# An attention kernel whose product with the values goes to 64x32 array tiles, from a rearranged weight tile

## The chip, the cores and the metric

One core of a Trainium2 chip runs the kernel. The metric is the device time of one execution in microseconds (us), as the median of several runs. The engines are TensorE (PE, with its weight loads shown apart as PEld), VectorE (DVE), ScalarE (ACT), GpSimd (POOL) and SyncE (SP, which only issues transfers here).

## The reference

A cross-attention block in float32. Two layer norms are modulated by a condition vector (adaLN), then queries come from x, keys and values from a context of 64 rows per batch element, and the block ends in a projection and a residual sum:

```
x: (16, 1024, 512)   context: (16, 64, 512)   16 heads of 32
xq  = LN(x)       * (1 + scale_q)  + shift_q      # scale, shift from silu(cond) @ Wss
xkv = LN(context) * (1 + scale_kv) + shift_kv
q = xq @ Wq + bq ;  k, v = split(xkv @ Wkv + bkv)
p = softmax(q k^T / sqrt(32))                     # over the 64 keys
out = x + (p v) @ Wp + bp
```

## The kernel before, in words

The 16 x 1024 rows are cut into 32 blocks (`NB`) of 512 rows, two to a batch element (`BPB`). Keys and values are made for the 16 batch elements in two context groups, A and B, in a prologue. Dense products (q, k, v, projection) are computed in 128x128 tiles by a scheme with seven products where a plain one has eight (`seven`, `product`). What belongs to a block i:

- `score_products` (L659-666): the scores of one half z of the keys (32 of 64) for all heads, K = 32, in 32x32 array tiles into two pairs of PSUM banks, `ps`. The pool `ps_s` holds just these two pairs, so the next score group, or the product with the values, needs both free again.
- `maximum` (L683, DVE), `copied` (L692, ACT: a pair of banks into the SBUF tile `s_tiles[i, z]`), `maxima` (L703, L712, tile mb on DVE), `subtract` (L725, POOL), `weights` (L731, ACT, the exponential in place).
- `total` (L765, POOL: both halves added), `row_total` (L770, DVE, tile lt), `inverse_rows` (L782-790): the reciprocal (L785) on DVE, then one transfer ltd<-lt to DRAM (L788) and four transfers vr<-ltd back (L790), all on SP; `spread_rows` (L796) spreads vr into vb.
- `mix` (L818-834): the product with the values into `po`, which takes the two bank pairs of `ps_s`. For each half z, each of four groups c of heads and each of four heads r in a group, one matmul with 32 rows (keys) and 32 columns; z = 1 accumulates on z = 0. So 32 matmuls, two instructions each. V lies in `V_A` or `V_B` with 32 partitions for each c, filled by `value_move` with transfers from `stage`.
- `divided` (L814, DVE, ot<-po,vb), `row_sums` (L928-938, POOL) and then the projection (`product`, L958).

The input of a later block is normalised by `q_stats`, `q_scale` (L310-319: five small ACT instructions, then four on POOL), `hidden` (L344), `turn` (L375) and `move` (L397: 16 transfers xt<-ht on SP), then `scale_features` (L455) and `feature_sums` (L506).

The order is written out by hand: a prologue, then a loop for i from 3 to 29 and a tail. Each engine works through its own instructions in that order. One pass of the loop holds, among others, `scores(i, 0, crossed=True)` (the two copies in swapped order), `scores(i, 1)`, `mix(i - 1)`, `weights(i, 0)`, `query_out(n, 6)`, `weights(i, 1)`, `total(i)`, `query_out(n, 7)`, `query_out(n, 3)`, `row_total(i)`, `inverse_rows(i)`, `move(i + 3)` and `q_scale(i + 4)`, with n = i + 1.

Of the kernel before, what the change touches and what calls it, by code (L numbers as in the profile page):

```python
# [15 lines left out]
P = 128  # L16
# [4 lines left out]
def cross_attention_block(  # L21
# [369 lines left out]
    def move(i, two=False):  # L391

        ht = ht_tiles.pop(i)
        xt = features_tile(i)
        for k in range(4):
            for g in range(4):
                (nc.gpsimd if two and g % 2 else nc.sync).dma_start(  # L397
                    xt[32 * k : 32 * k + 32, g],
                    ht[32 * g : 32 * g + 32, k].rearrange("p c t b -> p c (t b)"),
                )  # L400
# [258 lines left out]
    def score_products(i, z):  # L659
# [98 lines left out]

    sum_tiles, lt_tiles, vt_rows = {}, {}, {}
# [22 lines left out]
    def inverse_rows(i):  # L782

        lt = lt_tiles.pop(i)
        nc.vector.reciprocal(lt, lt)  # L785
        v = small.tile([P, NC, NJ], F32, tag="vr", name=f"vr_{i}")
        d = dram.tile([NC, 32, HPC, NJ], F32, tag="lt", name=f"ltd_{i}")
        nc.sync.dma_start(d.rearrange("c a r j -> (c a) r j"), lt)  # L788
        for r in range(HPC):
            nc.sync.dma_start(v[32 * r : 32 * r + 32], d[:, :, r, :].rearrange("c a j -> a c j"))  # L790
        vt_rows[i] = v
# [26 lines left out]
    def mix(i, apart=True, ks=(None,) * NC):  # L818
# [7 lines left out]
        else:  # L826
            po = [bank(f"po_{i}_{c}", ks[c]) for c in range(NC)]
            po_tiles[i] = po
        for z in range(2):
# [261 lines left out]
    q_stats("B", (2,))  # L1091
    turned_products()
    turned_scaled(3)
    load_x(1)
    q_stats("B", (1,))
    load_x(2)
    turned_scaled(2)
    context_out("A", "v", 7)
    context_product("A", "k", 5)
    column_sums("q", w_q_sb, w_q_sums, (0,))  # L1100
    column_sums("q", w_q_sb, w_q_sums, (1,))
    context_out("A", "v", 5)
    load_projection()
    q_stats("B", (3,))
    turned_scaled(0)
    context_product("A", "k", 4)
    context_out("A", "k", 4)
    q_scale("B")
    context_out("A", "k", 5)
    q_stats(1, (0,))  # L1110
    turned_scaled(1)
    hidden("B", (3,))
    context_product("A", "v", 3)
    hidden("B", (2,))
    context_product("A", "k", 3)
    hidden("B", (1,))
    turned_features("B", 1)
    turned_features("B", 3)
    q_stats(1, (1,))
    hidden("B", (0,))  # L1120
    feature_sums(0, nc.gpsimd, (0,))
    turned_features("B", 0)
    feature_sums(0, nc.gpsimd, (1,))
    turned_features("B", 2)
    column_sums("q", w_q_sb, w_q_sums, (2,))
    context_out("A", "k", 3)
    q_stats(1, (3,))
    query_product(0, 1)
    feature_sums(0, nc.gpsimd, (2,))
    modulated("B", 0, 0, nc.scalar)  # L1130
    q_stats(1, (2,))
    q_scale(1)
    query_seed(0)
    modulated("B", 1, 0, nc.vector)
    context_product("A", "v", 4)
    context_out("A", "v", 3)
    hidden(1, (0,))
    modulated("B", 0, 0, nc.vector)
    hidden(1, (1,))
    turn(1, (0,))  # L1140
    load_x(3)
    hidden(1, (2,))
    load_projection_bias()
    query_product(0, 2)
    turn(1, (1,))
    turn(1, (2,))
    hidden(1, (3,))
    column_sums("q", w_q_sb, w_q_sums, (3,))
    turn(1, (3,))
    q_stats(2, (0,))  # L1150
    feature_sums(0, nc.gpsimd, (3,))
    q_stats(2, (3,))
    context_out("A", "v", 4)
    move(1, two=True)
    query_out(0, 2)
    query_product(0, 6)
    query_out(0, 6)
    modulated("B", 0, 1, nc.scalar)
    modulated("B", 1, 1, nc.vector)
    modulated("B", 0, 1, nc.vector)  # L1160
    modulated("B", 1, 1, nc.scalar)
    context_product("B", "k", 1)
    query_product(0, 5)
    feature_sums("B", nc.gpsimd, (0,))
    context_out("B", "k", 1)
    query_product(0, 7)
    q_stats(2, (1,))
    modulated("B", 1, 0, nc.scalar)
    q_stats(2, (2,))
    feature_sums("B", nc.gpsimd, (1,))  # L1170
    query_out(0, 7)
    query_added(0, 5)
    context_product("B", "k", 2)
    query_product(0, 4)
    q_scale(2)
    q_stats(3, (0,))
    query_product(0, 3)
    context_out("B", "k", 2)
    q_stats(3, (2,))
    hidden(2, (0,))  # L1180
    hidden(2, (3,))
    feature_sums("B", nc.gpsimd, (2,))
    context_product("B", "k", 6)
    feature_sums("B", nc.gpsimd, (3,))
    hidden(2, (2,))
    query_out(0, 3)
    hidden(2, (1,))
    query_added(0, 4)
    q_stats(3, (1,))
    q_stats(3, (3,))  # L1190
    context_product("B", "k", 7)
    turn(2, (0,))
    turn(2, (1,))
    score_products(0, 0)
    scale_features(1, (1,))
    turn(2, (2,))
    context_out("B", "k", 6)
    context_out("B", "k", 7)
    value_move("A", 0)
    maximum(0, 0, 0)  # L1200
    context_product("B", "k", 5)
    scale_features(1, (0,))
    turn(2, (3,))
    copied(0, 0, 1)
    scale_features(1, (2,))
    maximum(0, 0, 1)
    context_product("B", "k", 4)
    copied(0, 0, 0)
    load_x(4)
    q_scale(3)  # L1210
    score_products(0, 1)
    scale_features(1, (3,))
    query_product(1, 1)
    context_out("B", "k", 5)
    context_out("B", "k", 4)
    context_product("B", "k", 3)
    maximum(0, 1, 0)
    maximum(0, 1, 1)
    maxima(0)
    move(2)  # L1220
    hidden(3, (0,))
    query_seed(1)
    context_out("B", "k", 3)
    feature_sums(1, nc.gpsimd, (0,))
    hidden(3, (2,))
    hidden(3, (1,))
    query_product(1, 2)
    feature_sums(1, nc.gpsimd, (1,))
    query_out(1, 2)
    copied(0, 1, 0)  # L1230
    feature_sums(1, nc.gpsimd, (2,))
    q_stats(4, (0,))
    subtract(0, zs=(0,))
    copied(0, 1, 1)
    q_stats(4, (2,))
    query_product(1, 6)
    context_product("B", "v", 1)
    turn(3, (0,))
    query_product(1, 7)
    turn(3, (1,))  # L1240
    value_move("A", 1)
    hidden(3, (3,))
    context_out("B", "v", 1)
    load_x(5)
    query_out(1, 6)
    query_out(1, 7)
    query_product(1, 5)
    weights(0, 0)
    query_added(1, 5)
    turn(3, (2,))  # L1250
    q_stats(4, (1,))
    subtract(0, zs=(1,))
    feature_sums(1, nc.gpsimd, (3,))
    weights(0, 1)
    context_product("B", "v", 2)
    scale_features(2, (3,))
    context_product("B", "v", 6)
    turn(3, (3,))
    scale_features(2, (2,))
    total(0)  # L1260
    scale_features(2, (0,))
    q_stats(4, (3,))
    context_out("B", "v", 2)
    q_scale(4)
    move(3)
    query_product(1, 3)
    query_product(1, 4)
    query_added(1, 4)
    context_out("B", "v", 6)
    query_out(1, 3)  # L1270
    scale_features(2, (1,))
    score_products(1, 0)
    row_total(0)
    copied(1, 0, 0)
    feature_sums(2, nc.gpsimd, (0,))
    maximum(1, 0, 1)
    context_product("B", "v", 5)
    maximum(1, 0, 0)
    inverse_rows(0)
    context_product("B", "v", 7)  # L1280
    nc.gpsimd.tensor_tensor(b_diff, b_second, b_first, ALU.subtract)
    context_out("B", "v", 7)
    copied(1, 0, 1)
    hidden(4, (1,))
    feature_sums(2, nc.gpsimd, (1,))
    score_products(1, 1)
    hidden(4, (2,))
    hidden(4, (0,))
    maximum(1, 1, 0)
    maximum(1, 1, 1)  # L1290
    maxima(1)
    query_product(2, 1)
    copied(1, 1, 0)
    context_out("B", "v", 5)
    copied(1, 1, 1)
    feature_sums(2, nc.gpsimd, (2,))
    scale_features(3, (3,))
    context_product("B", "v", 4)
    mix(0)
    q_stats(5, (0,))  # L1300
    turn(4, (0,))
    turn(4, (1,))
    feature_sums(2, nc.gpsimd, (3,))
    context_product("B", "v", 3)
    context_out("B", "v", 3)
    subtract(1, zs=(1,))
    subtract(1, zs=(0,))
    spread_rows(0)
    scale_features(3, (0,))
    query_seed(2)  # L1310
    query_product(2, 2)
    query_product(2, 6)
    biased(0, 2)
    context_out("B", "v", 4)
    hidden(4, (3,))
    query_out(2, 2)
    query_out(2, 6)
    query_product(2, 7)
    query_product(2, 5)
    weights(1, 1)  # L1320
    q_stats(5, (3,))
    query_out(2, 7)
    load_residual(0)
    divided(0)
    weights(1, 0)
    product(0, 1)
    query_added(2, 5)
    value_move("B", 0)
    product(0, 2)
    scale_features(3, (1,))  # L1330
    row_sums(0, 0)
    scale_features(3, (2,))
    q_stats(5, (1,))
    q_stats(5, (2,))
    query_product(2, 3)
    value_move("B", 1)
    total(1)
    turn(4, (2,))
    query_out(2, 3)
    load_x(6)  # L1340
    weight_sums(0)
    added(0, 1)
    added(0, 2)
# [305 lines left out]
```

## Time and profile before

| | |
|---|---|
| median of 3 runs (lowest, highest) | 1018.99 us (1018.93, 1021.01) |
| the profiled execution | 1021.49 us, span 1019.7 us, granted TensorE clock 0.999 |
| busy in the span | PE 1007.1 us, DVE 864.3, POOL 808.1, ACT 637.6 |
| moved by transfers | 149.82 MB, mean 147 GB/s |

The span runs from the first to the last instruction; the profiled execution's own time has 1.8 us around it. In rows of the timeline come the start, the length, the engine, the line, the operation, the tiles written and read, their shapes and how many instructions the row joins; in brackets stands the engine's idle time ahead of it and what ended that. Rows marked SPq are transfers being issued; their data land later.

### The profile page before, as it was taken

Reading aid. Unit: us, or ns where it says so; the run is one execution under the profiler, and the core shown is the slowest. Engines: PE = TensorE matmul, PEld = TensorE weight load, DVE = VectorE, ACT = ScalarE, POOL = GpSimd, SP = SyncE. Lnnn points to the kernel's source line nnn. Section 1 sums busy time; section 2 is a strip of 40 time slices with the busy share of each in tenths; the row PEclk is TensorE's granted clock in tenths of the full one; section 3 lists DMA queues with packets and bytes.
Section 4 is the critical chain, followed back from the end, with each engine's and each line's share of the span. In section 5 each row is a group of like instructions: output and inputs, shape, how many; then the busy total and the mean of one; then the engine's idle time right before and its main releaser. Section 6 shows DMA issues by size and latency. Waiting matters only on the chain.

```text
span 1019.7 us, 21289 instructions
## 1 busy us (share of the span) xinstructions
PE 1007.1 (99%) x8109; PEld 770.6 (76%) x8109; DVE 864.3 (85%) x1184; ACT 637.6 (63%) x1025; POOL 808.1 (79%) x518
## 2 busy tenths in 40 slices
PE   8999999999999999999999999999999999999997
PEld 7887777777777777777777777877777778777746
DVE  6787889898889888988898888889888888876785
ACT  3688666666667666666666666666666666565520
POOL 2659898888898888888987887898888888987781
PEclk9999999999999999999999999999999999999999
DMA  9574544444445544444454453444543444345122
GB/s 301 199 217 131 150 173 146 126 133 150 156 156 165 167 128 127 134 153 153 151 168 131 127 165 123 152 160 157 167 142 116 124 158 153 112 126 168 44 77 95
DMA packets 112117, 149.82 MB, mean 147 GB/s; under 512 B 34024, under 2 KB 45312, under 8 KB 112016
## 3 DMA queue, kind: packets, MB, share of 16 engines
q1 hardware_dynamic: 111760, 147.95, 45.6%
q8 instruction: 64, 1.05, 0.4%
q0 software_dynamic: 256, 0.52, 0.2%
q14 instruction: 37, 0.30, 0.1%
HBM read 79.21 MB, written 34.60 MB: 112 GB/s over the span
## 4 chain that ended last, share of the span: by engine, by line
PE 88%; DVE 3%; POOL 3%; DMA 2%; ACT 1%; SPq 1%; issue 1%; DVEq 0%; POOLq 0%; ACTq 0%
PE pp L958 35%; PE pq L547 35%; PE po L834 7%; PE ps L666 6%; POOL s L725 2%; PE pp L861 1%; PE pk_A L547 1%; PE pv_A L547 1%; PE pk_B L547 1%; SPq L397 1%; ACT s L731 1%; DVE m L683 1%; DMA wss_kv<-in_L_xcond_Wss_kv_dram 1%; DMA x<-in_x_dram 1%; DVE mb L712 0%
## 5 line engine op out<-in xcount | busy, mean ns | idle before, releaser
L725 POOL TENSOR_TENSOR s<-s,mb 128x2048 f32<-128x2048 f32 x64 | 290.3, 4561 | 128.1 <-DVE mb L712 128.1
L692 ACT COPY s<-ps 128x1024 f32<-128x1024 f32 x128 | 129.4, 1012 | 102.6 <-DVE m L683 59.4
L683 DVE TRANSPOSE_TENSOR_REDUCE m<-ps 128x32 f32<-128x1024 f32 x128 | 151.4, 1217 | 33.2 <-PE ps L666 33.1
L958 PE MATMUL pp<-w_p_sb,ot 128*128 128x256 f32 x736 | 169.4, 380 | 1.3 <-DVE ot L814 0.9
L982 DVE TENSOR_TENSOR r<-pp,r 128x512 f32<-128x512 f32 x210 | 136.6, 671 | 30.0 <-PE pp L958 24.9
L958 PEld LDWEIGHTS pp<-w_p_sb,ot 128*128 128x128 f32 x736 | 139.9, 190 | 21.8 <-issue 1.8
L586 ACT ACTIVATE qt<-pq,bias_t 128x256 f32<-128x256 f32 x256 | 105.6, 463 | 74.0 <-PE pq L547 74.0
L731 ACT ACTIVATE s<-s 128x2048 f32<-128x2048 f32 x64 | 122.4, 1912 | 46.3 <-POOL s L725 46.2
L765 POOL TENSOR_TENSOR sum<-s,s 128x2048 f32<-128x2048 f32 x31 | 140.7, 4540 | 4.4 <-ACT s L731 4.4
L958 PEld LDWEIGHTS pp<-WT,s 128*128 128x128 f32 x496 | 89.8, 190 | 56.7 <-issue 28.5
L547 PE MATMUL pq<-xt_sums,w_q_sums 128*128 128x256 f32 x512 | 123.6, 385 | 0.0
L958 PE MATMUL pp<-WT,s 128*128 128x256 f32 x496 | 123.0, 391 | 0.0
L547 PE MATMUL pq<-xt,w_q_sb 128*128 128x256 f32 x512 | 121.4, 380 | 0.0
L547 PEld LDWEIGHTS pq<-xt_sums,w_q_sums 128*128 128x128 f32 x512 | 95.3, 190 | 34.2 <-issue 22.6
L547 PE MATMUL pq<-xt,w_q_sums 128*128 128x256 f32 x512 | 121.1, 380 | 0.0
L958 PE MATMUL pp<-WT,ot 128*128 128x256 f32 x496 | 117.3, 380 | 0.0
L547 PEld LDWEIGHTS pq<-xt,w_q_sb 128*128 128x128 f32 x512 | 97.1, 190 | 16.1 <-issue 3.4
L547 PEld LDWEIGHTS pq<-xt,w_q_sums 128*128 128x128 f32 x512 | 97.4, 190 | 13.3 <-ACT qt L586 0.3
L958 PEld LDWEIGHTS pp<-WT,ot 128*128 128x128 f32 x496 | 94.3, 190 | 13.4 <-POOL WT L896 0.8
L344 ACT ACTIVATE x<-x,rstdq 128x512 f32<-128x512 f32 x128 | 97.0, 808 | 2.0 <-POOL rstdq L319 2.0
L455 ACT ACTIVATE xt<-xt,ss_q 128x512 f32<-128x512 f32 x124 | 94.3, 808 | 5.5 <-DMA xt<-ht 3.8
L301 DVE BATCH_NORM_STATS2 bs<-x 128x6 f32<-128x512 f32 x128 | 87.0, 680 | 0.3 <-DMA x<-in_x_dram 0.3
(176 smaller groups left out, 1488.8 us busy)
## 6 DMA issues: line engine op xcount, KB each, us to landing
x<-in_x_dram SPq DMA_DIRECT2D x32, 1024.0 KB, 5.4
r<-in_x_dram SPq DMA_DIRECT2D x32, 1024.0 KB, 5.1
xt<-ht SPq DMA_DIRECT2D x488, 64.0 KB, 2.0
out_dram<-r SPq DMA_DIRECT2D x60, 512.0 KB, 3.7
wss_q<-in_L_xcond_Wss_q_dram SPq DMA_DIRECT2D x4, 512.0 KB, 10.1
vr<-ltd SPq DMA_DIRECT2D x128, 8.0 KB, 1.6
out_dram<-r SPq DMA_DIRECT2D x7, 256.0 KB, 2.2
x_A<-in_ctx_dram SPq DMA_DIRECT2D x4, 256.0 KB, 3.0
```

What stands on the lines that cost most here:

```text
L301: nc.vector.bn_stats(bs, r)
L344: nc.scalar.activation(dst, src, AF.Identity, bias=rstd[:, 1, j : j + 1], scale=rstd[:, 0, j : j + 1])
L455: nc.scalar.activation(xt[:, :, c, :], xt[:, :, c, :], AF.Identity, scale=ss["q"][:, c, b : b + 1], bias=ss["q"][:, NC + c, b : b + 1],)
L547: nc.tensor.matmul(out_, lhsT=lhsT, rhs=rhs, start=new and m == 0 and c == 0, stop=c == HC - 1, skip_group_check=True,)
L586: nc.scalar.activation(dst, src, AF.Identity, bias=bq_t[:, o : o + 1])
L683: nc.vector.tensor_reduce(m_tiles[i][:, z, 2 * e : 2 * e + 2, :], s_banks[i, z][e].rearrange("p r (j a) -> p r j a", a=32), AX.X, ALU.max, ...
L692: nc.scalar.copy(s_tiles[i, z][:, 2 * e : 2 * e + 2, :], s_banks[i, z][e])
L725: eng.tensor_tensor(s_tiles[i, z], s_tiles[i, z], mb_tiles[i], ALU.subtract)
L731: nc.scalar.activation(p, p, AF.Exp, scale=SCALE)
L765: nc.gpsimd.tensor_tensor(t, s_tiles[i, 0], s_tiles[i, 1], ALU.add)
L958: nc.tensor.matmul(acc[k][:, t * HO : (t + 1) * HO], lhsT=rows[:, c, t * P : (t + 1) * P], rhs=cols[:, c, :], start=n == 2 and t == 0 and ...
L982: nc.vector.tensor_add(r, a, r)
```

## The change

For blocks 2 to 29 (`paired`) the product with the values is done with 64 rows (all keys of a batch element) and 32 columns to a matmul: 16 matmuls without accumulation in place of 32. This needs both halves of the keys of one head group in 64 neighbouring partitions, for the exponentials and for V. `swap` arranges the exponentials: six transfers per block, 32 partitions with 256 KB each, issued on ScalarE. Step 0 and step 1 fill a third tile `s_tiles[i, 2]` from the upper parts of the first and second tile; step 2 fills the upper parts of the first tile from the lower parts of the second, after `total` has read both. The second tile now has one fixed buffer (big1) and the third has big3. `value_move` writes V in the new layout, and for the first and last batch element in the old one also, with 24 transfers for each context group in place of 16. `move` and `inverse_rows` can be called in parts, and `load_residual` and `scale_features` stand at other places of the loop. The order of the prologue (about 350 lines) is written anew.

```diff
-    def value_move(i, m):
-        for c in (2 * m, 2 * m + 1):
-            for j in range(2):
-                for z in range(2):
-                    at = j * LKV + z * HK
-                    nc.sync.dma_start(
-                        V_all[i][32 * c : 32 * c + 32, j::2, z, :],
-                        stages[i][at : at + HK, :, c * P : (c + 1) * P],
-                    )
+    def value_move(i, c):
+        for j in range(2):
+            for z in range(2):
+                at = j * LKV + z * HK
+                src = stages[i][at : at + HK, :, c * P : (c + 1) * P]
+                p = 64 * (c // 2) + 32 * z
+                dst = V_all[i][p : p + 32, j::2, c % 2, :]
...
-            pool, tag = big, f"big{i % 2 * 2 + z}"
+            pool, tag = big, f"big{i % 2 * 2 if z == 0 else 3 if i == 1 else 1}"
...
+    def paired(i):
+        return BPB <= i < NB - BPB
+
+    def swap(i, step):
+
+        if not paired(i):
+            return
+        first, second = s_tiles[i, 0], s_tiles[i, 1]
+        if step == 0:
+            s_tiles[i, 2] = big.tile([P, HPC, TB], F32, tag="big3", name=f"s_{i}_2")
+        third = s_tiles[i, 2]
+        for at in (0, 64):
+            low, high = slice(at, at + 32), slice(at + 32, at + 64)
+            if step == 0:
+                nc.scalar.dma_start(third[low], first[high])
+            elif step == 1:
+                nc.scalar.dma_start(third[high], second[high])
+            else:
+                nc.scalar.dma_start(first[high], second[low])
...
+        if paired(i):
+            for c in (0, 2, 1, 3):
+                rows = slice(64 * (c // 2), 64 * (c // 2) + 64)
+                for r in range(HPC):
+                    nc.tensor.matmul(
+                        po[c][32 * r : 32 * r + 32, :],
+                        lhsT=vt[rows, c % 2, 32 * r : 32 * r + 32],
+                        rhs=s_tiles[i, 2 * (c % 2)][rows, r, :],
+                        start=True,
+                        stop=True,
+                    )
+            return
...
         weights(i, 0)
         query_out(n, 6)
-        scale_features(f, (0, 1))
+        swap(i, 0)
+        load_residual(i)
+        scale_features(f, (0,))
...
         weights(i, 1)
         total(i)
         query_product(n, 7)
         query_out(n, 7)
+        swap(i, 1)
+        scale_features(f, (1,))
         biased(a, 3)
         scale_features(f, (2, 3))
...
         query_product(n, 3)
         query_out(n, 3)
+        swap(i, 2)
         feature_sums(f)
         product(a, 7)
         row_total(i)
         inverse_rows(i)
```

More of the change, by code (lines that the diff above doesn't have):

```diff
@@ L1174, in cross_attention_block @@
+    move(1, two=True)
     query_product(0, 4)
     q_scale(2)
[L1176 to L1192 removed]
@@ L1236, in cross_attention_block @@
[L1236 to L1256, printed above, removed]
+    scale_features(1, (3,))
@@ L1335, in cross_attention_block @@
[L1335 to L1340, printed above, removed]
+    feature_sums(2, nc.gpsimd, (3,))
+    q_stats(5, (3,))
+    subtract(1, zs=(0,))
+    context_out("B", "v", 3)
+    load_residual(0)
+    spread_rows(0)
+    query_out(2, 7)
+    subtract(1, zs=(1,))
+    divided(0)
+    biased(0, 2)
+    row_sums(0, 0)
+    query_added(2, 5)
+    q_stats(5, (1,))
+    query_product(2, 4)
+    product(0, 1)
+    value_move("B", 2)
+    query_product(2, 3)
@@ L1341, in cross_attention_block @@
+    product(0, 2)
+    weights(1, 0)
+    weights(1, 1)
+    turn(4, (0,))
+    q_stats(5, (2,))
+    query_out(2, 3)
+    turn(4, (1,))
+    total(1)
+    query_added(2, 4)
+    turn(4, (2,))
+    q_scale(5)
+    query_product(3, 1)
+    added(0, 1)
+    turn(4, (3,))
+    query_seed(3)
+    added(0, 2)
+    value_move("B", 0)
     weight_sums(0)
-    added(0, 1)
-    added(0, 2)
-    query_product(2, 4)
+    value_move("B", 3)
     weight_sums(2)
-    turn(4, (3,))
-    query_added(2, 4)
-    query_product(3, 1)
@@ new lines, in cross_attention_block @@
+    maximum(2, 0, 0)
+    row_sums(0, 1)
+    weight_sums(3)
+    feature_sums(3, nc.gpsimd, (0,))
+    product(0, 7)
+    copied(2, 0, 1)
+    score_products(2, 1)
+    copied(2, 1, 1)
+    feature_sums(3, nc.gpsimd, (1,))
+    maximum(2, 1, 0)
+    maximum(2, 1, 1)
+    query_out(3, 2)
+    load_x(6)
+    product(0, 6)
+    added(0, 6)
+    move(4)
+    copied(2, 1, 0)
+    maxima(2)
+    hidden(5, (1,))
+    feature_sums(3, nc.gpsimd, (2,))
+    mix(1)
+    scale_features(4, (1,))
+    inverse_rows(1)
@@ L1427, in cross_attention_block @@
+    added(1, 1)
+    q_stats(6, (3,))
+    product(1, 2)
+    turn(5, (2,))
+    weights(2, 1)
+    scale_features(4, (2,))
+    added(1, 2)
+    load_x(7)
+    row_sums(1, 0)
+    turn(5, (3,))
+    total(2)
+    query_product(3, 3)
+    swap(2, 1)
+    biased(1, 3)
+    query_out(3, 3)
+    product(1, 7)
+    q_stats(6, (1,))
+    swap(2, 2)
+    row_total(2)
     row_sums(1, 1)
     feature_sums(4, nc.gpsimd, (0,))
+    inverse_rows(2)
     feature_sums(4, nc.gpsimd, (1,))
-    biased(1, 3)
```

456 lines of the change are left out of this document (226 added, 230 removed).

## The prediction

> **What bounds the kernel now.** I read the page first: the busy shares, then the chain that ended last.
>
> ```profile
> PE 1007.1 (99%) x8109; PEld 770.6 (76%) x8109; DVE 864.3 (85%) x1184; ACT 637.6 (63%) x1025; POOL 808.1 (79%) x518
> PE 88%; DVE 3%; POOL 3%; DMA 2%; ACT 1%; SPq 1%; issue 1%; DVEq 0%; POOLq 0%; ACTq 0%
> ```
>
> TensorE (PE) is busy 99% of the span and is 88% of the chain, so today a microsecond taken from PE is a microsecond won. ScalarE (ACT) is busy 63%; in a block of 29.2 us it seems to have 10 us to spare. Both shares are averages, so I went on to the timeline of one block: from the second score group of block 14 (479.19) to that of block 15 (508.38), 29.19 us. In it the product with the values is that of block 13; scores, softmax sums and row sums are block 14's.
>
> ```profile
> 479.19 1.14 PE L666 MATMUL ps<-qt,K_A 32*32 32x512 f32 x32
> 480.26 2.00 PE L958 MATMUL pp<-WT,s 128*128 128x256 f32 x8
> 482.09 1.89 PE L958 MATMUL pp<-w_p_sb,ot 128*128 128x256 f32 x8
> ...
> 483.57 2.31 DVE L712 STREAM_TRANSPOSE mb<-m 128x2048 f32<-128x2048 f32 x1
> 486.02 9.07 POOL L725 TENSOR_TENSOR s<-s,mb 128x2048 f32<-128x2048 f32 x2 [4.17 <-DVE mb L712]
> 487.36 2.35 PE L834 MATMUL po<-s,V_A 32*32 32x512 f32 x64
> 489.64 2.00 PE L547 MATMUL pq<-xt_sums,w_q_sums 128*128 128x256 f32 x8
> ...
> 495.05 1.29 POOL L928 TENSOR_TENSOR s<-ot 128x512 f32<-128x512 f32 x1
> 495.13 1.91 ACT L731 ACTIVATE s<-s 128x2048 f32<-128x2048 f32 x1 [0.47 <-POOL s L725]
> 496.42 1.27 POOL L929 TENSOR_TENSOR ot<-ot 128x512 f32<-128x512 f32 x1
> 497.66 4.53 POOL L765 TENSOR_TENSOR sum<-s,s 128x2048 f32<-128x2048 f32 x1
> 502.04 0.84 ACT L586 ACTIVATE qt<-pq,bias_t 128x256 f32<-128x256 f32 x2 [2.34 <-PE pq L547]
> 502.22 2.31 DVE L770 TRANSPOSE_TENSOR_REDUCE lt<-sum 128x64 f32<-128x2048 f32 x1 [0.34 <-POOL sum L765]
> 502.76 0.29 ACT L310 ACTIVATE workq<-mvq,eps_sb 128x4 f32<-128x4 f32 x1
> ...
> 503.72 0.19 ACT L315 ACTIVATE workq<-mvq 128x4 f32<-128x4 f32 x1
> 504.57 0.55 DVE L785 RECIPROCAL lt<-lt 128x64 f32<-128x64 f32 x1
> 505.01 1.01 ACT L692 COPY s<-ps 128x1024 f32<-128x1024 f32 x1 [1.10 <-PE ps L666]
> 505.15 0.34 SPq L788 DMA_DIRECT2D ltd<-lt  x1
> 506.26 1.01 ACT L692 COPY s<-ps 128x1024 f32<-128x1024 f32 x1 [0.24 <-DVE m L683]
> 508.38 1.14 PE L666 MATMUL ps<-qt,K_A 32*32 32x512 f32 x32
> 508.48 1.75 SPq L790 DMA_DIRECT2D vr<-ltd  x4
> ```
>
> Three things are to be seen. First, the product po holds PE from 487.36 to 489.64, 2.28 us. Second, a chain of other engines runs beside PE with hardly a gap from the score group at 479.19 through the maximum, its spread mb, the subtraction, the two row sums of ot (L928, L929), the total, lt and the reciprocal, which ends at 505.12: 25.93 us after the scores. PE does not wait for its end; the next scores of the second half come at 508.38 by PE's own order. Third, ACT finishes its five small q_scale instructions (L310 to L315) and the two copies that free the score banks (L692, ending at 507.27) some 1.1 us before PE wants those banks at 508.38. That is all the slack ACT has at this place, whatever its 63% says.
>
> **The product in 64x32 tiles.** Before, 64 instructions in 32x32 tiles, so four rounds of the 16 tiles; after, 32 instructions in eight tiles, again four rounds, without accumulation. A lower bound for the new time: eight dense matmuls of 256 columns take 482.09 - 480.26 = 1.83 us, 0.46 for 512 columns, so four rounds take 1.83 and the gain is 0.45. An upper bound: the score group, 32 instructions in two rounds, holds PE 480.26 - 479.19 = 1.07; twice that is 2.14 and the gain 0.14. No row has the 64x32 shape; the score group's 1.07 plus two rounds at 0.46 is 1.98, or 1.91 as the mean of that and 1.83, and I take a gain of 0.37. For 28 blocks that is 10.4 us (3.9 to 12.6), if PE stays the bound.
>
> The Trainium skill speaks against that gain: "TensorEngine Tiling (Array Packing)", section "Theoretical Speedup", gives up to 2x for dimensions up to 64 and up to 4x up to 32, so that half as many tiles of twice the rows do the work in the same time, and the gain would be 0.
>
> **The swaps' issues.** Six transfers a block go out on ACT. SP's issues of like shape (32 partitions) stand in for them:
>
> ```profile
> L397 SPq DMA_DIRECT2D xt<-ht x488: 507/589/1884, 54.3 to 929.7; - x163
> L788 SPq DMA_DIRECT2D ltd<-lt x32: 320/345/526, 101.6 to 993.8; - x32
> DMA to landing us min/median/max: 1.5/1.5/3.4
> L790 SPq DMA_DIRECT2D vr<-ltd x128: 318/424/1256, 103.2 to 997.0; - x128
> DMA to landing us min/median/max: 1.5/1.6/3.4
> ```
>
> At 0.59 each, six are 3.5 us of ACT. Steps 0 and 1 (two each, after query_out 6 and 7) fall before 502.04, where ACT idles 2.34 us, and the total does not wait for them: its start is held by POOL's own row sums until 497.69, and the second exponential ends at 497.04. I cost them at nothing, at most 0.5 us of later exponential; if that cover went, 1.2 us a step. The residual load moved behind step 0 and the 16 more moves of V touch SP only in stretches where it has nothing due: nothing. The prologue in its new order has no row; context group B has eight more moves on SP, 8 x 0.59 = 4.7 us later if all of it fell on the path, and as much sooner if its old moves stood there; I take 0.
>
> **The wait that step 2 brings.** This decides the forecast. In the changed kernel as built, every transfer signals on one of eight counters taken in turn, and waits, on the engine that issues it, until the counter's last user has landed. The built order around step 2 of block i is: ltd; vr 1, 2, 3; first transfer of step 2; vr 4; three xt moves; second transfer of step 2. The second one is the eighth after vr 1 of the same block, shares its counter, and so waits for it. I find this for 27 blocks, 2 to 28 (for block 2 it is vr 2; block 29 waits for an old one). No data needs it. vr 1 in turn waits for ltd, ltd for the reciprocal. Behind the waiting issue stand, in ACT's order, q_scale and both copies of the next block's first score banks; PE's second score group needs those banks. So the chain that ran free until now closes on itself, from second scores to second scores:
>
> - scores to reciprocal 25.93, and 0.03 to ltd's issue at 505.15;
> - ltd's issue to vr 1's issue: the timeline's rows of SP, below;
> - vr 1 from issue to landing: 1.6 (the median);
> - the held issue 0.59;
> - q_scale 502.76 to 503.91: 1.15;
> - the two copies, without their gaps: 2.02, with releases of 0.3 in all, an estimate from the 0.24 in front of the second copy.
>
> ```profile
> 155.23 0.34 SPq L788 DMA_DIRECT2D ltd<-lt  x1
> 156.74 1.28 SPq L790 DMA_DIRECT2D vr<-ltd  x3
> ...
> 945.19 0.34 SPq L788 DMA_DIRECT2D ltd<-lt  x1
> 946.67 1.75 SPq L790 DMA_DIRECT2D vr<-ltd  x4
> ```
>
> These are the first and the last of 28 such pairs. SP stands still between them, 1.48 us in the last: the issuer is what waits. In 20 of the 28 the step is 1.47 to 1.86, in eight 3.06 to 3.59, as at 505.15 above; the mean is 2.05. That gives 25.96 + 2.05 + 1.6 + 0.59 + 1.15 + 2.02 + 0.3 = 33.67 us a block, against 29.19: 4.48 more, and 27 of them are 121 us. With every step at its best (1.47, and an issue at 0.51) it is 33.0, 103 us; with ltd always slow (3.3) it is 34.9, 155 us. PE's 0.37 does not come off: po is not on this chain, PE merely idles longer. The profiled run took 1021.5, the median of the runs is 2.5 lower; against the median, 1019 + 121 = 1140.
>
> The Trainium skill, "DMA: Bandwidth & Descriptors", section "Anatomy of one DMA — SWDGE (gpsimd) path", says that a DMA engine does not wait on semaphores and that the wait is made by the sequencer that issues, before dispatch; the SP rows above agree. Were it otherwise, ACT would run on and the first rival's time would come out.
>
> **Rivals.**
> 1. *The wait does not bite*: vr 1 has landed, or q_scale and the copies are not held, before ACT gets there. Then PE bounds, the price is the product's gain alone: 1019 - 10.4, about 1 us given back where the exponentials come late: 1010 (1006 to 1017). It decides if vr 1 has landed by 508.38 less release, copies, q_scale and issue (0.3 + 2.02 + 1.15 + 0.59), that is by 504.32 in this frame; the reciprocal alone ends at 505.12. For it stands only that the trace shows no wait of this kind on ACT. Faster; chance 0.07.
> 2. *The swaps also stretch ltd and vr*: the first transfer of step 2 moves 256 KB at the moment ltd goes out, and both land at the 3.4 of the rows' maximum each time. 25.96 + 3.4 + 3.4 + 4.06 = 36.8, 7.6 more, 206 us: 1225. For it: the eight slow ltd. Against: rows with large transfers in flight still have medians of 1.5 and 1.6. Chance 0.09.
> 3. *Nothing happens*: four rounds cost the same in both shapes, and no wait: 1019 with 1 to 2 us of prologue, 1018 to 1022. The score group's 1.07 for two rounds speaks half for it. Chance 0.03.
>
> **How the numbers follow.** The forecast, closing of the chain at 33.0 to 34.9 us, has 0.81: 1140. Slower is 0.81 + 0.09 and half of the third rival, 0.91; faster is the first, 0.07; same is the rest, 0.02 (0.2% is about what a measurement of this kernel can tell from no change). For the range I take the chain's ends, 1122 and 1174, and widen them by its unknown parts: if most of q_scale's 1.15 can be done ahead of the wait it is 1.0 us a block less than its best, 27 us: 1095 below; if part of the stretching of rival 2 comes, 0.3 us a block more, 8 us: 1182 above. Rivals 1 and 3 and the full rival 2 stay out, under 0.2 together.
>
> **What would show it.** Right: second scores of neighbouring blocks 33 to 35 us apart in blocks 3 to 29, PE busy near 88%, ACT's small L310 group starting behind vr 1's landing and 1 us or more after the first score group, po's slot at 1.8 to 2.1 us. The counter theory is wrong if L310 starts within 1.5 us of query_out 3 while vr 1 is still out; the chain's sum is wrong if the time between scores and reciprocal is no longer 25.9 us; the product's gain is wrong if po still holds PE 2.2 us. All is wrong if the blocks come 29 us apart.

## The result, and the profile after

The changed kernel takes 1218.81 us in the median (1215.56 to 1221.74), against 1019.68 for four runs of the kernel before: the ratio is 1.195, 95% interval 1.1916 to 1.1985. The forecast was 1140 with a range up to 1182; the sign was right, the size was not. The profiled execution took 1221.74 us, its span is 1219.4. Medians below are of all runs of a kernel, ratios of the runs within 1.5% of its fastest; one single run, of the kernel with step 2 on GpSimd, lies outside that.

From the page of the changed kernel: the busy shares, the chain that ended last, and two rows of the transfer issues (KB each, median us from issue to landing).

```profile
PE 1067.6 (88%) x7213; PEld 793.5 (65%) x7213; DVE 871.1 (71%) x1184; ACT 641.7 (53%) x1025; POOL 808.7 (66%) x518
PE 28%; POOL 19%; issue 16%; DVE 13%; DMA 12%; ACT 5%; SPq 5%; ACTq 1%; POOLq 0%; DVEq 0%
...
s<-s ACTq DMA_DIRECT2D x168, 256.0 KB, 4.9
x<-in_x_dram SPq DMA_DIRECT2D x32, 1024.0 KB, 8.4
```

TensorE was 88% of the chain and is 28% now; in its place stands a ring through POOL, DVE and transfers. TensorE has 896 instructions fewer and is yet busy 60 us longer, which the forecast did not have. From the waits view (total us, times, longest):

```profile
ACT workq L310 <- DMA vr<-ltd: 200.5, 26, 10.4
DVE m L691 <- ACT s L700: 171.7, 28, 8.5
PEld ps L674 <- ACT s L700: 148.6, 28, 7.9
```

These three are the forecast's wait, in its order: ScalarE stands ahead of q_scale until vr has landed (26 blocks, 7.7 us each), its copies come late, and TensorE's second score group waits for them. The timeline of one such place:

```profile
562.77 0.51 ACTq L785 DMA_DIRECT2D s<-s  x1
564.16 1.14 PE L674 MATMUL ps<-qt,K_A 32*32 32x512 f32 x32
565.12 0.55 DVE L815 RECIPROCAL lt<-lt 128x64 f32<-128x64 f32 x1
565.70 0.34 SPq L817 DMA_DIRECT2D ltd<-lt  x1
568.98 1.75 SPq L827 DMA_DIRECT2D vr<-ltd  x4
570.61 0.52 ACTq L785 DMA_DIRECT2D s<-s  x1
571.17 0.30 ACT L310 ACTIVATE workq<-mvq,eps_sb 128x4 f32<-128x4 f32 x1 [7.79 <-DMA vr<-ltd]
572.22 1.90 ACT L700 COPY s<-ps 128x1024 f32<-128x1024 f32 x2
574.18 2.33 PE L674 MATMUL ps<-qt,K_A 32*32 32x512 f32 x32 [5.23 <-ACT s L700]
576.24 2.38 DVE L691 TRANSPOSE_TENSOR_REDUCE m<-ps 128x32 f32<-128x1024 f32 x2 [0.57 <-PE ps L674]
576.44 3.65 PE L1007 MATMUL pp<-WT,s 128*128 128x256 f32 x8
580.13 0.69 DVE L1031 TENSOR_TENSOR r<-pp,r 128x512 f32<-128x512 f32 x1 [1.51 <-PE pp L1007]
580.74 0.28 DVE L711 TENSOR_REDUCE m<-m 128x64 f32<-128x128 f32 x1
585.20 1.95 PE L870 MATMUL po<-s,V_A 64*32 64x512 f32 x32
587.08 1.99 PE L548 MATMUL pq<-xt_sums,w_q_sums 128*128 128x256 f32 x8
```

The two transfers of step 2 are 7.84 us apart; the second goes out 1.63 us after the first vr, that is when it has landed. The product holds TensorE for 587.08 - 585.20 = 1.88 us (2.28 before). What is new: the score group at 574.18 takes 2.33 us where it took 1.14, and the eight matmuls after it 3.65 where they took 2.00. The view by windows gives the granted clock (PEclk) over the wait and after it:

```profile
core 0: us, PE busy (x) PEld busy (x) DVE busy (x) ACT busy (x) POOL busy (x), PEclk, DMA share, GB/s
564.15:573.20 9.05, 4.80 (x49) 3.19 (x48) 2.59 (x3) 1.97 (x7) 6.83 (x9) 0.99 0.50 127
573.20:576.40 3.20, 2.22 (x32) 0.46 (x32) 2.58 (x4) 1.41 (x3) 0.14 (x1) 0.50 0.41 106
576.40:580.20 3.80, 3.80 (x18) 3.09 (x11) 2.29 (x3) 2.56 (x3) 0.00 (x0) 0.55 0.43 106
580.20:587.00 6.80, 6.80 (x56) 4.61 (x54) 6.50 (x6) 3.36 (x7) 3.49 (x1) 1.00 0.16 40
```

After 5.23 us without work TensorE has half its clock granted until shortly before 580.2, and that is where its added busy time comes from. VectorE's residual sum (580.13) waits for those slow matmuls, and the last step of the maximum (580.74) stands behind it in VectorE's order. The same two rows of the kernel before, in the block that the prediction shows:

```profile
482.69 0.65 DVE L982 TENSOR_TENSOR r<-pp,r 128x512 f32<-128x512 f32 x1
483.26 0.27 DVE L703 TENSOR_REDUCE m<-m 128x64 f32<-128x128 f32 x1
```

The last step of the maximum came 4.07 us after the start of the scores (483.26 - 479.19); here it comes 6.56 us after it.

### The profile page after: what moved, and what is told of

It reads as the page before. It is cut to its first block, busy times and chain, and to the rows that moved or that the text cites. A ratio compares the mean times of both kernels' runs of the same rounds, so it can differ in the third digit from the quotient of the medians.

```text
span 1219.4 us, 19834 instructions
## 1 busy us (share of the span) xinstructions
PE 1067.6 (88%) x7213; PEld 793.5 (65%) x7213; DVE 871.1 (71%) x1184; ACT 641.7 (53%) x1025; POOL 808.7 (66%) x518
## 4 chain that ended last, share of the span: by engine, by line
PE 28%; POOL 19%; issue 16%; DVE 13%; DMA 12%; ACT 5%; SPq 5%; ACTq 1%; POOLq 0%; DVEq 0%
PE pp L1007 12%; POOL sum L793 9%; DMA ltd<-lt 7%; PE pq L548 6%; PE ps L674 5%; DVE lt L798 5%; POOL s L733 4%; DVE mb L720 4%; ACT s L700 3%; SPq L398 3%; DMA vr<-ltd 3%; POOL s L977 2%; POOL ot L978 1%; PE pp L910 1%; DVE lt L815 1%
## 5 line engine op out<-in xcount | busy, mean ns | idle before, releaser
L691 DVE TRANSPOSE_TENSOR_REDUCE m<-ps 128x32 f32<-128x1024 f32 x128 | 154.7, 1228 | 192.1 <-ACT s L700 171.7
L700 ACT COPY s<-ps 128x1024 f32<-128x1024 f32 x128 | 126.1, 1007 | 103.6 <-DVE m L691 84.1
L1007 PE MATMUL pp<-w_p_sb,ot 128*128 128x256 f32 x736 | 172.3, 384 | 1.3 <-DVE ot L851 0.9
L1007 PEld LDWEIGHTS pp<-WT,s 128*128 128x128 f32 x496 | 114.6, 242 | 87.7 <-DVE r L1031 43.8
L1007 PE MATMUL pp<-WT,s 128*128 128x256 f32 x496 | 161.4, 482 | 0.0
L1007 PEld LDWEIGHTS pp<-w_p_sb,ot 128*128 128x128 f32 x736 | 143.9, 196 | 24.0 <-issue 1.8
L310 ACT ACTIVATE workq<-mvq,eps_sb 128x4 f32<-128x4 f32 x32 | 9.5, 298 | 210.8 <-DMA vr<-ltd 200.5
L456 ACT ACTIVATE xt<-xt,ss_q 128x512 f32<-128x512 f32 x124 | 97.3, 809 | 39.7 <-issue 35.0
L674 PE MATMUL ps<-qt,K_A 32*32 32x512 f32 x1024 | 51.7, 775 | 68.8 <-ACT s L700 68.8
L674 PE MATMUL ps<-qt,K_B 32*32 32x512 f32 x1024 | 52.4, 780 | 68.0 <-ACT s L700 68.0
```

The lines of the kernel that those rows point to most:

```text
L456: nc.scalar.activation(xt[:, :, c, :], xt[:, :, c, :], AF.Identity, scale=ss["q"][:, c, b : b + 1], bias=ss["q"][:, NC + c, b : b + 1],)
L674: nc.tensor.matmul(pss[r // 2][32 * c : 32 * c + 32, r % 2, :], lhsT=kt[rows, c, z * HK : (z + 1) * HK], rhs=qt[rows, c, :], start=True, s ...
L691: nc.vector.tensor_reduce(m_tiles[i][:, z, 2 * e : 2 * e + 2, :], s_banks[i, z][e].rearrange("p r (j a) -> p r j a", a=32), AX.X, ALU.max, ...
L700: nc.scalar.copy(s_tiles[i, z][:, 2 * e : 2 * e + 2, :], s_banks[i, z][e])
L1007: nc.tensor.matmul(acc[k][:, t * HO : (t + 1) * HO], lhsT=rows[:, c, t * P : (t + 1) * P], rhs=cols[:, c, :], start=n == 2 and t == 0 and ...
```

## The experiments

All ratios are against the kernel before, run on the same chip.

**The wait alone.** The kernel before, with one small transfer per block on ScalarE that needs the first vr.

```diff
+        if 2 <= i <= 28:
+            seen = small.tile([1, NC * NJ], F32, tag="seen", name=f"seen_{i}")
+            nc.scalar.dma_start(seen, v[0:1].rearrange("p c j -> p (c j)"))
```

> The kernel before, unchanged but for one small transfer per block (1 partition, 64 bytes of vr) that ScalarE issues for blocks 2 to 28 behind the first vr transfer, whose landing it has to wait for; it moves next to nothing. Theory A: this wait alone makes nearly all of the loss: 25.96 + 2.05 (ltd as before) + 1.6 + 0.55 + 1.15 + 2.0 + 0.3 = 33.6 us a block and the 2.5 us of the slowed TensorE on top, 36.1: 1019 + 27 x 6.9 = 1206, 1120 (without the 2.5) to 1220. Theory B: no bytes, no loss: 1019 to 1022.

Measured: 1167.13 us, ratio 1.1444 (1.1427 to 1.1461). The timeline shows the same picture as the changed kernel, with next to no bytes:

```profile
569.32 0.34 SPq L788 DMA_DIRECT2D ltd<-lt  x1
571.76 1.75 SPq L790 DMA_DIRECT2D vr<-ltd  x4
573.36 0.51 ACTq L794 DMA_DIRECT2D seen<-vr  x1
573.92 0.30 ACT L310 ACTIVATE workq<-mvq,eps_sb 128x4 f32<-128x4 f32 x1 [6.53 <-DMA vr<-ltd]
576.93 2.33 PE L666 MATMUL ps<-qt,K_A 32*32 32x512 f32 x32 [3.97 <-ACT s L692]
```

The time lies in the expected range, 39 us under the 1206 that were expected. So the wait by itself makes 148 of the 199 us. The mean distance of second score groups over blocks 3 to 27 is 34.75 us (29.29 before, 36.58 in the changed kernel).

**TensorE kept at work through the wait.**

```diff
-        query_product(n, 1)
+        for _ in range(4):
+            query_product(n, 1)
```

> The changed kernel with one of the query products (eight matmuls into a bank that it starts anew) done four times instead of once in each pass of the loop, so that TensorE works through the 5.2 us in which it otherwise waits for ScalarE's copies: 27 x 3 x 1.9 us of added work of no use. The wait for vr is kept. Theory C: 2.5 us of each block's 36.9 come from TensorE running at a lower granted clock after its idle time, which delays the maximum behind it on VectorE; then blocks come about 34.5 us apart and the time falls to 1150, 1140 to 1175, with more work. Rival: the delay on VectorE has another cause (its order alone); then the time stays at 1219 or rises by up to 10.

Measured: 1185.56 us, ratio 1.1628 (1.1606 to 1.1649): 33 us less than the changed kernel, with 27 x 3 x 8 = 648 more matmul instructions. TensorE's rows:

```profile
580.41 8.04 PE L548 MATMUL pq<-xt,w_q_sb 128*128 128x256 f32 x32
588.38 1.14 PE L674 MATMUL ps<-qt,K_A 32*32 32x512 f32 x32
589.46 1.99 PE L1007 MATMUL pp<-WT,s 128*128 128x256 f32 x8
```

The score group is back at 1.14 us and the matmuls after it at 1.99; the reciprocal ends 25.94 us after the scores in the mean, as before (28.17 in the changed kernel). The theory holds; the fall is half of what was expected, because the filling was too long: the second scores now wait for it, 1.05 us behind the copies in the mean, where they followed them at 0.05.

**The new product alone, and the new order alone.**

```diff
-            pool, tag = big, f"big{i % 2 * 2 if z == 0 else 3 if i == 1 else 1}"
+            pool, tag = big, f"big{i % 2 * 2 + z}"
...
-        if not paired(i):
-            return
+        return
...
-                        rhs=s_tiles[i, 2 * (c % 2)][rows, r, :],
+                        rhs=s_tiles[i, c % 2][rows, r, :],
```

> The product in 64x32 tiles alone: no swap is issued, the matmuls read the tiles as they lie (the wrong keys for half the heads), and the exponential tiles have their old buffers. Prologue and loop order are those of the changed kernel. The product's slot of 1.88 us in the changed kernel's trace against 2.28 before gives 0.40 x 28 = 11 us less where TensorE bounds: 1008 us, 1006 to 1012. If the shape brings nothing where TensorE bounds, 1019.

Measured: 1013.61 us, ratio 0.9957 (0.9941 to 0.9972). For the order alone, `paired` is also set to False:

> The changed kernel's prologue, loop order and moves of V with the old product in 32x32 tiles and no swap (V lies where the new product wants it, so the product reads wrong values). In the run of the new product alone, the second scores of block 3 came 3.1 us later than before and the loop's 25 blocks saved 11.3: so 3 us slower than before is expected here, 1022, 1020 to 1024; 1019 if the lateness came with the product.

Measured: 1022.33 us, ratio 1.0033 (1.002 to 1.0046). The difference of the two, 8.7 us (give or take 2, by the intervals), is what the new shape brings in 28 blocks; the new order gives 3 us back.

**Step 2 on SyncE.**

```diff
-                nc.scalar.dma_start(first[high], second[low])
+                nc.sync.dma_start(first[high], second[low])
```

> Only the two transfers of step 2 are issued on SyncE instead of ScalarE; bytes, tiles, product and order are those of the changed kernel. In the built order the second of them now shares its counter with a transfer of step 0 of the same block, landed long before. Theory A (ScalarE held by the wait for vr): the hold ahead of L310 is gone, TensorE is the bound again with the shorter product, blocks about 28.8 us apart, 1008 to 1014 us. Theory B (the 44 MB of swaps, beside ltd and vr and the loads, make the block long): nothing changes, 1200 us or more. A stretched ltd, about 3 us from issue to vr, would be seen in both and would cost nothing under A.

Measured: 1125.62 us, ratio 1.103 (1.0999 to 1.1062). The hold ahead of L310 is gone, but the time is far from 1010: theory A alone falls here. From ltd's issue to vr's it takes 5.9 us in the mean. The next runs ask whether that is SyncE's queue.

**Step 2 on GpSimd, or one transfer of it.** The same line with `nc.gpsimd`; in the second run only for the upper half (`at` = 64).

> The two transfers of step 2 are issued on GpSimd, right behind the total that they wait for anyway; all else is the changed kernel's. In the built order they wait only for step 0 of the same block, ScalarE waits for no vr, and ltd has SyncE's queue to itself. Theory A with its refinement (in the run with step 2 on SyncE ltd stood behind 512 KB in one queue, 5.9 us, and with it vr and the xt moves behind vr): blocks 28.8 to 29.5 us apart, 1010 to 1030 us. Theory B (44 MB more cost time wherever they are issued): 1100 us or more, as with step 2 on SyncE.

> Of step 2 the first transfer stays on ScalarE, the second is issued on GpSimd. In the built order neither waits for vr. As above: theory A 1010 to 1030 us, theory B 1100 or more. If GpSimd's issue of both costs its chain something, this one is the faster of the two.

Measured: 1118.11 us, ratio 1.0951 (1.0921 to 1.0982), and 1127.85, ratio 1.1071 (1.1057 to 1.1086). Neither is near 1030, and the mixed one is not the faster. From the run with both on GpSimd, SyncE's rows of one block, the ScalarE row that takes xt, and two rows of its waits:

```profile
515.96 0.38 SPq L109 DMA_DIRECT2D x<-in_x_dram  x1
523.25 0.34 SPq L817 DMA_DIRECT2D ltd<-lt  x1
529.48 1.75 SPq L827 DMA_DIRECT2D vr<-ltd  x4
531.34 10.03 SPq L398 DMA_DIRECT2D xt<-ht  x16
544.89 0.81 ACT L456 ACTIVATE xt<-xt,ss_q 128x512 f32<-128x512 f32 x1 [4.45 <-DMA s<-s]
```

```profile
ACT xt L456 <- DMA s<-s: 62.2, 12, 7.4
ACT xt L456 <- DMA xt<-ht: 30.4, 11, 6.2
```

vr goes out 6.23 us after ltd (1.5 in most blocks of the kernel before), the xt moves behind it as much later, and ScalarE, which takes xt first of all, waits for transfers. The swaps issued on ScalarE and the xt moves share the eight counters, so the transfer named in a row can be the wrong one of the two. Followed by counter and time of landing, the wait ahead of 544.89 ends with the sixteenth xt move, landed at 544.74, and of the 25 such waits from block 3 on that end with a transfer (100 us in all) 21 with 83 us end with an xt move. The load of x takes 10.8 us in the median (5.4 in the kernel before).

**Fewer bytes in step 2, and hardly any in all steps.**

```diff
-                nc.scalar.dma_start(first[high], second[low])
+                nc.scalar.dma_start(first[high, 0, :8], second[low, 0, :8])
```

> All six transfers on ScalarE, but the two of step 2 carry 32 bytes a partition in place of 8 KB (the upper parts of the first tile keep the wrong keys). Their built order changes with it: the second now waits for a transfer of step 1 instead of vr. 1 MB of swaps a block is left, and ScalarE issues as much as before. Theory A: 1008 to 1018 us. If the issues or the bytes of steps 0 and 1 cost time on their own, over 1030.

> All six transfers of a block are issued on ScalarE at their places, but each carries 32 bytes a partition in place of 8 KB, so that next to no bytes move (the product reads the first tile twice and gives wrong values). In the built order no one waits for vr. If ScalarE's six issues cost nothing, the time is that of the product alone, 1013.6: 1011 to 1018. If the issues hold ScalarE too long, over 1022.

Measured: 1049.26 us, ratio 1.0295 (1.026 to 1.033), and 1015.31, ratio 0.9964 (0.9949 to 0.9978). Six issues a block on ScalarE cost nothing that shows (1013.61 without them); the bytes do.

**Where the load of x stands.** Four runs move the load of x, or ltd, to see what makes ltd late. In the first the load goes behind ltd and vr, and all swaps stay on ScalarE:

```diff
-        if i < NB - 5:
-            load_x(i + 5)
...
         inverse_rows(i)
+        if i < NB - 5:
+            load_x(i + 5)
...
         if i + 3 < NB:
             move(i + 3)
```

> The changed kernel with one line moved: the load of x five blocks ahead (1 MB on SyncE) goes out behind ltd and vr instead of some 7 us ahead of them. All six swaps stay on ScalarE. By this the built order changes so that the second transfer of step 2 waits for a transfer of step 1 in place of vr. Theory D: in the runs without the wait for vr the time of about 1120 came from ltd standing in SyncE's queue behind this load, which the swaps stretch from 5.4 to 10.8 us; vr and then the xt moves go out 4.5 us late, and ScalarE, and TensorE behind it, wait for xt. Then ltd to vr falls from 6.1 to about 2 us. The seventh xt move now shares its counter with the load and waits for it, so some of the moves are still late by 2 to 5 us: 1020 to 1080 us. Without D (the bytes cost time wherever the load stands): 1110 or more.

Measured: 1118.34 us, ratio 1.0981 (1.092 to 1.1042); ltd to vr 3.3 us in the mean, the moves still late behind the load, as SyncE waits for the load's counter at the seventh. ScalarE's wait is shorter, but not gone: it idles 59.9 us in all ahead of L310 (210.8 in the changed kernel). The time is outside the expected range. In the next two the load stands between the halves of the moves, once with step 2 on ScalarE and once with it on GpSimd:

```diff
-        if i < NB - 5:
-            load_x(i + 5)
...
         if i + 3 < NB:
-            move(i + 3)
+            move(i + 3, range(2))
+        if i < NB - 5:
+            load_x(i + 5)
...
+        if i + 3 < NB:
+            move(i + 3, range(2, 4))
```

> As the run before, but the load of x goes out between the eighth and the ninth xt move. In this built order the second transfer of step 2 waits for the first vr again. So the wait on ScalarE is kept, and only what stood in SyncE's queue ahead of ltd is gone. Theory A with D: the block is that of the small transfer that only waited for vr, 34.8 us, and the time its 1167 us (1150 to 1185); ltd to vr 1.6 us in place of 3.2. If the difference between 1219 and 1167 came from the swaps' bytes in another way: 1200 or more.

Measured: 1184.03 us, ratio 1.1609 (1.1579 to 1.1639); ltd to vr 1.98 us, blocks 35.0 us apart. The time is inside the expected range, at its upper end: of the 52 us between the wait alone and the changed kernel, 35 go with the place of the load. A block is 1.56 us shorter; 1.24 us of that lie between ltd and vr, and scores to reciprocal, at 27.75, gives 0.42.

> Step 2 on GpSimd (no wait for vr) and the load of x between the eighth and the ninth xt move. Theory D: ltd to vr about 2 us, moves on time but for the last, blocks 28.8 to 30 us apart: 1012 to 1040. Without D: 1110 or more.

Measured: 1071.0 us, ratio 1.0513 (1.0481 to 1.0545); ltd to vr 2.99 us. Half of the loss is gone, but the time is not in the range. In the fourth run the load of x stays, step 2 is on GpSimd, and ltd changes its engine and goes behind q_scale:

```diff
-        nc.sync.dma_start(d.rearrange("c a r j -> (c a) r j"), lt)
+        nc.scalar.dma_start(d.rearrange("c a r j -> (c a) r j"), lt)
...
         row_total(i)
+        if i + 4 < NB:
+            q_scale(i + 4)
         inverse_rows(i)
...
```

> Step 2 on GpSimd, the load of x where it was, but ltd issued on ScalarE, behind q_scale, so that it stands in another queue than the load of x. If ltd is late because it stands behind the load in one queue: ltd to vr about 2 us and 1015 to 1050. If it is late because all queues share the same 16 engines: ltd to vr still 5 to 6 us, 1110 or more.

Measured: 1112.55 us, ratio 1.0915 (1.0884 to 1.0945). ltd now has ScalarE's queue, and vr still goes out 6.36 us later:

```profile
520.67 0.33 ACTq L817 DMA_DIRECT2D ltd<-lt  x1
...
527.03 2.37 SPq L827 DMA_DIRECT2D vr<-ltd  x4
```

So ltd is not late because the load of x stands ahead of it in its own queue. It is late while that load (10.3 us in this run) and the swaps of step 2 are in flight: in this block ltd lands at 527.01, the load at 526.46, and the two swaps, issued on GpSimd, at 526.07 and 526.82.

**The xt moves first.** Step 2 on GpSimd, and SyncE's order changed.

```diff
-        if i < NB - 5:
-            load_x(i + 5)
...
+        if i + 3 < NB:
+            move(i + 3, range(2))
         row_total(i)
         inverse_rows(i)
+        if i < NB - 5:
+            load_x(i + 5)
...
         if i + 3 < NB:
-            move(i + 3)
+            move(i + 3, range(2, 4))
```

> Step 2 on GpSimd (no wait for vr); the first eight xt moves go out ahead of ltd, as soon as their buffer is free, then ltd and vr, the load of x, and the other eight moves. All swaps and bytes as in the changed kernel. Theory D': without the wait for vr the loss is only that xt lands after ScalarE wants it, because the moves wait behind ltd and vr, which wait behind bulk transfers. With half the moves early the last is issued some 4 us sooner than with the load of x in the middle (1071 us): 1013 to 1040. If the bytes cost time through something else than the moves: 1065 or more.

Measured: 1033.67 us, ratio 1.012 (1.0101 to 1.014). All bytes are there, and 84 of the 98 us are gone. Of these, 47 came with the load of x moved (1071.0), and 37 with the first eight moves put ahead of ltd, the one thing in which these two runs differ. From block 3 to block 4 alone it is 37.36 us: the prologue still issues the moves for that block late.

> The run before with the prologue in the order of the kernel before (the moves of V in the new layout, the swaps of block 2 put in). The order alone made the new prologue 3.2 us slower, so this is 3 us below the run before, if the 16 more moves of V are hidden: 1010 to 1037 us.

Measured: 1038.22 us, ratio 1.0183 (1.017 to 1.0196): 4.5 us slower in place of 3 faster. With the old order it is 36.1 us from block 1 to block 2 and 35.7 from 3 to 4 (29.6 and 37.4 in the run before): that prologue seems not to hide the added moves of V and the swaps of block 2; no run takes them apart.

**And once more, in the loop and the prologue.** Step 2 on GpSimd; the lines of the loop (the prologue's are changed in the same way):

```diff
-        if i < NB - 5:
-            load_x(i + 5)
...
+        if i + 3 < NB:
+            move(i + 3, (0,))
         row_total(i)
+        inverse_out(i)
+        if i + 3 < NB:
+            move(i + 3, (1,))
         inverse_rows(i)
         if i + 3 < NB:
-            move(i + 3)
+            move(i + 3, (2,))
+        if i < NB - 5:
+            load_x(i + 5)
...
+        if i + 3 < NB:
+            move(i + 3, (3,))
```

> All six swaps with their bytes, step 2 on GpSimd, and SyncE's order rewritten once more, in the loop and ahead of it: four xt moves, ltd, four moves while ltd lands, vr, four moves, the load of x, the last four. In the run with eight early moves block 4 alone was 8 us long, because the moves for it were still issued late by the prologue; the rest of the loop averaged 29.3. Expected: that block's 8 us gone and vr on time: 1019 to 1027 us. If the lateness has another cause than the moves' and vr's place: 1033 again.

Measured: 1018.18 us (12 runs, 1013.69 to 1022.26), ratio 0.9978 (0.9963 to 0.9994).

```profile
504.06 2.93 SPq L398 DMA_DIRECT2D xt<-ht  x4
505.57 1.14 PE L674 MATMUL ps<-qt,K_A 32*32 32x512 f32 x32
507.04 1.07 POOL L785 DMA_DIRECT2D s<-s  x2
507.47 0.35 SPq L817 DMA_DIRECT2D ltd<-lt  x1
507.86 2.83 SPq L398 DMA_DIRECT2D xt<-ht  x4
510.29 1.14 PE L674 MATMUL ps<-qt,K_A 32*32 32x512 f32 x32
510.80 2.10 SPq L827 DMA_DIRECT2D vr<-ltd  x4
512.94 2.41 SPq L398 DMA_DIRECT2D xt<-ht  x4
515.45 0.53 SPq L109 DMA_DIRECT2D x<-in_x_dram  x1
516.02 2.44 SPq L398 DMA_DIRECT2D xt<-ht  x4
```

vr goes out 3.33 us after ltd, four moves fill that time, and the last move goes out by 518.46, 8.2 us after the second scores. (In the kernel before, in the block that ends at 508.38, the moves began behind vr, at 510.32, 1.94 us after the second scores, and took 11.35 us.) From block 3 to block 4 it is now 29.64 us, and from block 10 on the blocks are 28.8 us apart, the value of the new product alone. The control is the kernel before with this order in the loop:

> The kernel before (old product, no swaps, its own prologue) with the same order on SyncE in the loop. It tells what that order is worth without the swaps: the kernel before loses about 0.1 us a block (29.29 in the mean against 29.18) where xt lands late, so 1016 to 1019 us. If the order itself costs something, over 1021, and that cost is in the run beside it too.

Measured: 1019.1 us, ratio 0.9993 (0.9984 to 1.0001): the order brings nothing that shows without the swaps. So a version with the new product and all 44 MB of swaps stands 0.2% below the kernel before: the product's gain, less what the prologue and the first blocks give back.

## Why the prediction was wrong in size and right in kind

**The wait, right.** The second transfer of step 2 is held by vr in 26 blocks and ends the chain as forecast. The wait alone, put into the kernel before, makes it 14% slower.

**The sum of the chain, wrong by 2.9 us a block.** Term by term, forecast against the mean over blocks 3 to 27 of the changed kernel:

- scores to reciprocal: 25.93 against 28.17. This is the step that failed most, and the prediction had named it as a sign of being wrong. The forecast took the chain of the other engines from the trace of before as it stood, and noted only that "PE merely idles longer". But behind each of these idle times TensorE worked at half its clock, and a part of the chain runs through it: scores, then the matmuls that VectorE's residual sum waits for, ahead of the last step of the maximum. The run that kept TensorE at work brought the 25.94 back.
- ltd's issue to vr's: 2.05 against 3.22. This step failed too: the rows of before were taken for the changed kernel, while the swaps lie beside ltd. With the wait but next to no bytes it was 1.63, with the load of x moved 1.98.
- vr's issue to the end of the held issue (1.6 + 0.59): 2.19 against 2.15. q_scale and the copies: 3.17 against 2.95. Releases: 0.3 against 0.05.

Together 33.67 against 36.58, and 27 blocks by 2.9 us are the 79 us between 1140 and 1219. TensorE's busy share came out at the 88% that was forecast by luck: it was busy 60 us longer in a span that was longer too.

**The second rival, near in time and half right in kind.** Its 1225 is close to what was measured, which is luck in part. It had ltd and vr both at 3.4: for ltd that was right (3.22), but the first vr landed in 1.56 us in the mean, and the clock, which it did not have, made up for that.

**The product, right.** The slot is 1.88 us (forecast 1.91), 0.40 less than before. With the wait it was forecast to be worth nothing; no run tests that alone, but the blocks of 35.02 us with the new product, the wait and the load of x moved are not shorter than the 34.75 of the old product with the wait alone. Without wait and bytes it is worth 8.7 us (forecast 10.4, bounds 3.9 to 12.6). The Trainium skill's table in "TensorEngine Tiling (Array Packing)", section "Theoretical Speedup", by which nothing would be won, is not borne out here: 32 instructions without accumulation hold TensorE 0.40 us less than 64 with it. Which of the two differences makes the gain, the shape or the missing accumulation, was not taken apart.

**"I cost them at nothing", right for the issues, wrong for the bytes.** Six issues cost nothing (1015.3 with hardly any bytes). The 1.5 MB a block were not priced at all. Without the wait they cost about 100 us over the kernel before, through ltd, vr and the xt moves behind vr; in the changed kernel a part of that lay behind the longer wait, since the wait's 148 and these 100 together made 199. So the first rival's 1010 was wrong too: with the wait for vr gone, all bytes in place and the load of x ahead of ltd, four kernels came out at 1113 to 1128. That the moves are the path is shown by the runs that send them earlier and keep every byte (1071.0 to 1033.7, then 1018.2).

**The prologue, inside its bounds.** Taken at 0, bounds of 4.7 both ways; it cost 3.

**What stays open.** Of the 52 us between the wait alone and the changed kernel, 17 are left when the load of x is moved. In the profiled runs 11 of them lie ahead of block 3, whose second scores come at 172.27 us against 161.28, and 7 in blocks 3 to 27; what makes the 11 was not taken apart. That ltd lands late beside the bulk transfers was shown for two queues; why it does was not.

## What to carry to other kernels

A transfer put on a compute engine's queue can bring a wait of its own: look in the built order for the transfer whose completion counter it shares, and list what stands behind it on that engine. When a chain closes, do not carry its links over from the old trace: ask of each what the new idle time, above all TensorE's, and the new traffic beside it will do. Bytes that seemed cheap on average hurt here through a small transfer that had to land at once (ltd). Sending the load behind it and the moves that can go early ahead of it won 84 us; the choice of its queue won 6 at most (1118.1 against 1112.6).

## What the runs showed of the hardware

In blocks 3 to 27 of the changed kernel TensorE stood idle for 3.8 to 7.5 us ahead of the second scores, and each time a stretch at a granted clock of 0.50 came with it: 3.41 us in seven blocks, 6.83 in seventeen, 10.24 in one. The full clock was back 3.4 to 4.2 us after the first score matmul in the seven and 5.2 to 6.7 us after it in the others. A score group of 1.14 us took up to 2.33, and some 6 us of needless matmuls in the gap made the kernel 33 us faster. In the run with the wait alone, gaps of 2.9 to 4.7 us were enough. The Trainium skill has the rule, in "TensorE: Matmul & The Clock Gate", section "Part 1: The HAM clock gate (the "warmup" mystery)": half the rate after an idle window of some 3.4 us, and full rate after a busy one as long. The trace agrees in that the stretches are 3.41 us or a multiple of it, though a gap of 2.9 us brought one too. The rule was there to be used in the forecast, and by the measured 2.2 us a block the slow clock is worth 60 of the 79 us that were missing.

A transfer of 32 KB (ltd) landed in 1.49 us in the median in the kernel before. Beside the load of x and the swaps of step 2 on GpSimd it took 5.6 us from SyncE's queue and 6.0 from ScalarE's. It took both: ltd's issue to vr's was 1.87 us with the load and no swaps, 2.99 with the swaps and the load moved, 6.07 with the two together. The Trainium skill, "DMA: Bandwidth & Descriptors", section "Issuing engines are not separate DMA queues", says that transfers of all issuing engines run on the same 16 engines; the run with ltd on ScalarE agrees.
